# Sums of weights, first norm, last ELU and the place of the h^T reads in a two-layer graph attention kernel

## Chip, cores and metric

The kernel runs on one core of a Trainium2 chip. The metric is the device time of one launch in microseconds (us), the median of three runs. One more run was made under the profiler; every duration below is from that execution.

## What is computed

For each of 64 graphs (256 nodes, 512 channels, float32) two layers are applied, each on the normed and rectified input, each added to it. Layer 0 is gated multi-head attention under an adjacency mask, layer 1 graph attention with one head and an ELU.

```python
# layer 0, h = relu(layernorm(x)), 8 heads of 64
q, k, v = h @ Wq.T, h @ Wk.T, h @ Wv.T
attn = softmax(where(adj != 0, q k^T / 8, -inf)); c = attn @ v
gate = sigmoid(concat([c, h]) @ Wg.T + bg)
x = x + gate * h + (1 - gate) * c
# layer 1, h = relu(layernorm(x))
Wh = h @ W; e = leaky_relu(Wh @ a1 [:, None] + Wh @ a2 [None, :], 0.2)
x = x + elu(softmax(where(adj == 0, -1e9, e)) @ Wh)
```

## The kernel before

Work goes by graph. Graph g is loaded, normed (`p_...`), multiplied to q, k and v, attended (`a_...`), gated and sent through layer 1 (`g_...`). Five graphs are in flight at once: `emit_round(i)` issues, in an order written out by hand, a bit of graph p = i + 1 (its norm, q, k, v and scores), of i (its softmax and weighted sum), of q = i - 1 (gate, residual, second norm), of r = i - 2 (W h, edge logits, output) and of o = i - 3 (ELU and store). The rounds run from -1 to 63, and `emit_end` writes out what is left. Nothing is reordered: each engine executes its instructions in the order in which these functions call them, and so does SyncE (SP), whose queue issues every DMA. An instruction that waits holds all that stand behind it on its engine.

Each 512-wide product is cut by Strassen's scheme (`strassen`, L163): seven products "1" to "7" of half-size blocks are accumulated in three PSUM banks, and steps named "u1", "u2", "u3", "c00" to "c11" take sums off the banks (L190 on VectorE, L192 on ScalarE). The scheme needs sums of token blocks (`token_sums`, L151, on GpSimd, four a call) and, once per weight, sums of weight blocks (`weight_sums`, L108). A weight's four sums are, in their order, the factor of product 7, that of 6, that of 5 (in place) and that of 4. For q and k they run on VectorE ahead of the first graph's product "6"; for v on GpSimd; for the gate's two weights (gh, gc) and for W they are put in a list of 21 `chores` (4 + 4 sums, one scaling of the bias, 8 edge columns L137, 4 sums), which `chore(chores, n)` takes off n at a time at places in the rounds.

What is called h^T is h with channels on partitions. From graph FIRST = 3 on it is made by three steps: VectorE turns 32 x 32 blocks (`turn`, L244), SP writes them to DRAM in four DMAs (`p_send`, L253), and reads them back in four others, in another order (`p_fetch`, L260). For the first three graphs TensorE transposes instead. The attention weights e take the same way: `a_turn` (L391), `a_send` (L397, one write for each of four quarters of a graph), `a_fetch` (L402, four reads for each). In a round the calls that SP sees around the change are: h^T write of p, first, second, third and fourth write of e of i, h^T read of p, first read of e.

x is loaded by `load_graph` (L92) in one DMA, the adjacency by `load_edges` (L98) into a single buffer, so that the next graph's load waits on SP until `p_mask` (L227) has read the one before. At the start SP issues x, the weights q and k, the adjacency and v. The first norm (`p_stats` ... `p_norm`, L201 to L218) takes both 128-row tiles through each step together.

The ELU of layer 1 is made of `g_neg` (VectorE L635: the negative part, out of PSUM), `g_pos` (ScalarE L640 the positive part, L641 the exponential), `g_elu` (L646) and `g_add` (L651, on GpSimd, for the last graphs but one on VectorE). In the last graph `g_add_first` and `g_add_last` (L656, L660) take the place of the last two. In `emit_end`, a = 63, b = 62, c = 61 and o = 60. The tiles of ELU come from the pool `tmp` (5 buffers).

Of the kernel before, what the change touches and what calls it, by code (L numbers as in the profile page):

```python
# [22 lines left out]
def kernel(  # L23
# [65 lines left out]
    def load_graph(g):  # L89
        xt = sb["x"].tile([P, NT, H], F32, tag="t", name=f"x_{g}")  # L90
        at = sb["adj"].tile([P, NT, N], I32, tag="t", name=f"adj_{g}")
        nc.sync.dma_start(xt, x[g].rearrange("(t p) h -> p t h", p=P))  # L92
        graphs[g] = {"x": xt, "adj": at}
        if g > 0:
            load_edges(g)
# [9 lines left out]
        for n in range(2):  # L105
            eng.dma_start(w[:, :, n, :HH], sources[key][:, n * HH:(n + 1) * HH].rearrange("(c p) f -> p c f", p=P))

    def weight_sums(key, eng=None):  # L108

        w = weight[key]  # L110
        t = const.tile([P, 3, 2, w.shape[3]], F32, name=f"w{key}_t")
        b11, b12, b21, b22 = (w[:, r:r + 2, n, :] for r in (0, 2) for n in range(2))
        weight[key] = {1: b11, 2: b21, 3: b22, 4: t[:, 2], 5: b12, 6: t[:, 0], 7: t[:, 1]}
        eng = eng or nc.vector
        return [lambda args=args: eng.tensor_tensor(*args) for args in (
            (t[:, 1], b22, b12, ALU.subtract),
            (t[:, 0], t[:, 1], b11, ALU.add),
            (b12, b12, b11, ALU.subtract),
            (t[:, 2], b21, t[:, 0], ALU.subtract),
        )]  # L120
# [116 lines left out]

    def p_norm(g):
        graphs[g]["h"] = norm_relu(graphs[g], f"l0_{g}")

    def turn(h):

# [381 lines left out]
    def g_out(g, t):  # L624
        s = graphs[g]
        pm = s["po", t] = ps["w"].tile([P, H], F32, tag="t", name=f"po_{g}_{t}")
        for kc in range(NT):
            nc.tensor.matmul(  # L628
                pm, s["egT"][:, t, kc, :], s["wh"][kc][:, :, :HH], start=(kc == 0), stop=(kc == NT - 1)
            )  # L630

    def g_neg(g, t):
        s = graphs[g]
        neg = s["neg", t] = sb["tmp"].tile([P, H], F32, tag="t", name=f"neg_{g}_{t}")
        nc.vector.tensor_scalar(neg, s["po", t], s["rec1"][:, t:t + 1], 0.0, ALU.mult, ALU.min)  # L635

    def g_pos(g, t):
        s = graphs[g]
        pos = s["pos", t] = sb["tmp"].tile([P, H], F32, tag="t", name=f"pos_{g}_{t}")
        nc.scalar.activation(pos, s.pop(("po", t)), AF.Relu, scale=s["rec1"][:, t:t + 1])  # L640
        nc.scalar.activation(s["neg", t], s["neg", t], AF.Exp)  # L641

# [4 lines left out]

    def g_add(g, t):
        s = graphs[g]
        eng = nc.vector if g >= B - 4 else nc.gpsimd  # L650
        eng.tensor_tensor(s["x"][:, t, :], s["x"][:, t, :], s.pop(("pos", t)), ALU.add)  # L651

    def g_add_first(g, t):
# [21 lines left out]
    def emit_round(i):  # L675


        p, q, r, o = i + 1, i - 1, i - 2, i - 3

        def do(fn, g, *args):  # L680
            if 0 <= g < B:
                fn(g, *args)

        def run(fn, g, steps):

            if fn is g_gate and i == 0:
                fn, g = p_qk, p
            elif fn is g_wh and i == 0:
                fn, g = p_v, p
            if 0 <= g < B:  # L690
                if (fn, g) not in products:
                    products[fn, g] = fn(g), set()
                product, done = products[fn, g]
                for step in steps.split():
                    if step not in done:
                        product(step)
                        done.add(step)

        def stats():
            do(p_stats, p + 1, 0)  # L700
            do(p_stats, p + 1, 1)
            do(p_root, p + 1)

        def scores():
            do(a_scores, p, 0)
            do(a_scores, p, 1)
            do(g_out, r, 0)
            do(g_out, r, 1)
            do(a_max, p, 0, 0)
            do(p_bias, p + 1)  # L710
            do(a_exp, p, 0, 0, 0)
            do(a_max, p, 0, 1)
            do(a_exp, p, 0, 0, 1)
            do(p_norm, p + 1)
            do(a_max, p, 1, 0)
            do(a_max, p, 1, 1)
            do(g_fetch_h, q)
            do(a_scale, p, 0, 0)
            do(a_exp, p, 0, 1, 0)
            do(a_exp, p, 0, 1, 1)  # L720
            do(g_neg, r, 0)


        if i == 0:
            do(p_sums, p)
        run(g_gate, q, "1")
        do(g_neg, o, 1)
        do(p_send, p)
        do(g_pos, o, 0)
        run(g_gate, q, "u1")  # L730
        do(a_scale, i, 0, 1)
        do(a_turn, i, 0, 0, 0)
        do(a_turn, i, 0, 0, 1)
        do(a_send, i, 0, 0)
        do(a_exp, i, 1, 0, 0)
        do(a_exp, i, 1, 0, 1)
        do(a_turn, i, 0, 1, 0)
        run(g_gate, q, "6 u2")
        do(a_turn, i, 0, 1, 1)
        do(a_send, i, 0, 1)  # L740
        if i <= B:
            do(g_sums_h, r)
        do(g_elu, o, 0)
        run(g_gate, q, "5")
        do(a_scale, i, 1, 0)
        do(g_pos, o, 1)
        run(g_gate, q, "7 u3 c11")
        do(a_exp, i, 1, 1, 0)
        do(a_exp, i, 1, 1, 1)
        do(a_scale, i, 1, 1, True)  # L750
        do(a_turn, i, 1, 0, 0)
        do(a_turn, i, 1, 0, 1)
        do(a_send, i, 1, 0)
        do(a_turn, i, 1, 1, 0)
        do(g_diff, q)
        run(g_gate, q, "2 c00 4 c10")
        do(g_tanh, q, 0)
        do(a_turn, i, 1, 1, 1)
        do(a_send, i, 1, 1)
        do(p_fetch, p)  # L760
        do(p_mask, p)
        chore(chores, 2)
        run(g_gate, q, "3 c01")
        do(a_fetch, i, 0, 0)
        do(g_mix, q, 0, True)

        run(g_wh, r, "1 u1")
        do(g_tanh, q, 1)
        do(g_mix, q, 0, False)
        run(g_wh, r, "6 u2 5")  # L770
        do(g_mix, q, 1, True)
        run(g_wh, r, "7 u3 c11")
        do(g_mix, q, 1, False)
        chore(chores, 2)
        run(g_wh, r, "2 c00 4")
        if i != 0:
            do(p_sums, p)
        do(g_turn, q)
        do(g_send, q)
        do(a_fetch, i, 0, 1)  # L780
        run(g_wh, r, "c10 3 c01")
        if i == B - 1:
            return
        do(g_fetch, q)
        do(a_fetch, i, 1, 0)

        if i == -1:
            chore(weight_sums("q"), 4)
            chore(weight_sums("k"), 4)
        run(p_qk, p, "1 u1")  # L790
        do(g_edges, r)
        do(g_logits, r)
        do(g_leaky, r)
        run(p_qk, p, "6 u2 5")
        do(g_elu, o, 1)
        do(g_add, o, 1)
        do(g_add, o, 0)
        do(g_store, o)
        do(g_exp, r)
        do(g_turn_e, r)  # L800
        do(g_send_e, r)
        do(g_rec, r)
        run(p_qk, p, "7 u3 c11 2 c00")
        do(load_graph, p + 1)
        if i == -1:
            for key in ("gh", "gc", "1"):
                load_weight(key, nc.sync)
            load_small()
            chores.extend(weight_sums("gh") + weight_sums("gc"))
            chores.append(lambda: nc.vector.tensor_scalar_mul(hbg, hbg, 0.5))  # L810
            chores.extend(edge_columns() + weight_sums("1"))
        chore(chores, 1)
        do(a_fetch, i, 1, 1)
        do(g_fetch_e, r)
        do(g_residual, q, 0)
        run(p_qk, p, "4 c10")
        do(g_residual, q, 1)
        chore(chores, 1)
        run(p_qk, p, "3 c01")
        chore(chores, 1)  # L820
        do(g_stats, q, 0)
        if i == -1:
            chore(weight_sums("v", nc.gpsimd), 4)
            stats()
            scores()
        run(p_v, p, "1 u1 6 u2")
        do(g_stats, q, 1)
        do(g_root, q)
        run(p_v, p, "5 7 u3 c11")
        do(g_bias, q)  # L830
        do(g_norm, q)
        run(p_v, p, "2 c00")
        chore(chores, 1)
        do(g_turn_h, q)
        do(g_send_h, q)
        run(p_v, p, "4 c10")
        chore(chores, 1)
        run(p_v, p, "3 c01")
        chore(chores, 1)
        if i >= 0:  # L840
            stats()
        do(g_sums, i)

        do(a_weigh, i, 0)
        do(a_evac, i, 0)
        do(a_weigh, i, 1)
        do(a_evac, i, 1)
        do(a_sums, i)
        if i >= 0:
            scores()  # L850
        do(p_turn, p + 1)
# [7 lines left out]
    def emit_end():  # L859
# [99 lines left out]
        for t in range(NT):  # L959
            g_elu(b, t)  # L960
            g_add(b, t)
        g_store(b)
        for t in range(NT):
            g_neg(a, t)
            g_pos(a, t)
            g_add_first(a, t)
        for t in range(NT):
            g_add_last(a, t)
            g_store(a, t)

    with tc.manual_schedule(engines={getattr(mybir.EngineType, e) for e in ("PE", "SP", "Pool", "DVE", "Activation")}):
# [3 lines left out]
        load_edges(0)  # L975
        wake_up()
        load_weight("v", nc.sync)
        p_stats(0, 0)
        p_stats(0, 1)
        for fn in (p_root, p_bias, p_norm, p_transpose_pe):  # L980
            fn(0)
        for i in range(-1, B):
            emit_round(i)
            graphs.pop(i - 4, None)
# [33 lines left out]
```

## Time and profile before

| | |
|---|---|
| median of 3 runs | 3174.41 us (3173.53 to 3177.22) |
| the profiled execution's own time | 3178.26 us |
| its span in the profile | 3176.5 us |
| TensorE busy (matmuls) | 3125.6 us, 98% |
| VectorE busy | 2473.4 us, 78% |
| GpSimd, ScalarE busy | 1507.0 us, 1415.1 us |
| DMA | 589.59 MB, 186 GB/s in the mean |
| chain of work that ended last | TensorE 88%, VectorE 5%, DMA 3% |

The profile has a page with busy times, and views that answer questions: who waited for whom, the instructions in order of time (timeline), busy times by stretch. In the timeline a line is: start in us, duration in us (from the first to the last instruction where several are merged), engine, source line, operation, what it writes <- what it reads, shapes, count, and in brackets the engine's idle time before it and what ended that. PE is TensorE's matmuls, PEld its weight loads, DVE VectorE, ACT ScalarE, POOL GpSimd, SPq the issue of a DMA by SyncE. A round is measured here from one graph's first score matmul (L343) to the next graph's. The shortest are 48.29 us; the 60 rounds from 174.10 to 3087.50 us take 2913.4 us.

### The profile page before, as it was taken

The numbers are of one execution on the slowest core, as the hardware profiler recorded it, in microseconds if no ns is written. First come the engines' busy times: TensorE is split into PE (matmuls) and PEld (weight loads), VectorE is DVE, ScalarE is ACT, GpSimd is POOL, SyncE is SP. The second block draws the span as 40 slices with busy tenths as digits, with TensorE's granted clock in tenths as the row PEclk, the third lists the DMA queues.
The fourth block names the chain that finished last, engine by engine and source line by source line (L and its number), as shares of the span: only waits on it lengthen the run. The fifth ranks groups of instructions, "written<-read, shape, count | busy, mean of one in ns | idle before, by whom it ended". The sixth has DMA issues, their size and how long they took to land.

```text
span 3176.5 us, 66771 instructions
## 1 busy us (share of the span) xinstructions
PE 3125.6 (98%) x22768; PEld 2725.1 (86%) x22768; DVE 2473.4 (78%) x6369; ACT 1415.1 (45%) x3977; POOL 1507.0 (47%) x2179
## 2 busy tenths in 40 slices
PE   7899999999999999999999999999999999999997
PEld 6888889888888888898898888888988988888886
DVE  6777877877878778778778787777787787877776
ACT  2443544544435434445445354344454453443443
POOL 3444544545545445445455354454454554544543
PEclk9999999999999999999999999999999999999999
DMA  5577778787787787787777877877878778778772
GB/s 169 155 173 204 181 185 200 185 191 199 177 203 189 176 209 183 183 202 186 193 198 179 199 186 182 208 181 182 203 185 193 197 180 199 189 178 209 184 169 80
DMA packets 1098163, 589.59 MB, mean 186 GB/s; under 512 B 681568, under 2 KB 1024096, under 8 KB 1097824
## 3 DMA queue, kind: packets, MB, share of 16 engines
q1 hardware_dynamic: 1097824, 585.32, 74.4%
q8 instruction: 183, 3.00, 0.4%
q14 instruction: 156, 1.28, 0.1%
HBM read 304.35 MB, written 280.76 MB: 184 GB/s over the span
## 4 chain that ended last, share of the span: by engine, by line
PE 88%; DVE 5%; DMA 3%; POOL 2%; SPq 1%; issue 1%; ACT 1%; DVEq 0%; ACTq 0%; POOLq 0%
PE pmb_qk L179 10%; PE pmb_z L179 9%; PE pma_qk L179 7%; PE pmc_qk L179 7%; PE pc L423 7%; PE ps L343 6%; PE pma_z L179 6%; PE pmc_z L179 6%; PE po L628 6%; PE pmb_v L179 5%; PE pmb_wh L179 5%; PE pmc_v L179 3%; PE pma_v L179 3%; PE pmc_wh L179 3%; PE pma_wh L179 3%; DVE e L358 1%
## 5 line engine op out<-in xcount | busy, mean ns | idle before, releaser
L367 ACT ACTIVATE e<-e,low 128x256 f32<-128x256 f32 x1024 | 506.4, 499 | 66.1 <-DVE low L358 66.1
L209 POOL TENSOR_TENSOR rs_l<-ve_l,mhalf 128x2 f32<-128x2 f32 x128 | 89.2, 697 | 887.5 <-DVE ve_l L205 887.5
L358 DVE CUSTOM_DVE_ANT_0 e<-ps,mask 128x256 f32<-128x256 f32 x1024 | 362.2, 416 | 104.7 <-PE ps L343 104.7
L382 POOL TENSOR_SCALAR e<-e,rec 128x256 f32<-128x256 f32 x768 | 354.5, 482 | 151.5 <-DVE rec L375 101.9
L391 DVE STREAM_TRANSPOSE eb<-e 128x512 f32<-128x512 f32 x512 | 351.4, 696 | 78.0 <-POOL e L382 65.3
L218 ACT ACTIVATE h_l<-x,nb_l,rs_l 128x512 f32<-128x512 f32 x256 | 194.1, 805 | 220.2 <-DVE nb_l L213 126.0
L157 POOL TENSOR_TENSOR S_l<-hT_l 128x256 f32<-128x256 f32 x128 | 93.9, 733 | 397.7 <-DMA hT_l<-there_h 351.6
L423 PE MATMUL pc<-eT,v 128*64 128x256 f32 x2048 | 238.3, 384 | 7.3 <-DMA eT<-there_e 7.1
L343 PE MATMUL ps<-qk 64*128 64x256 f32 x2048 | 240.0, 384 | 0.9 <-DVE qk L190 0.9
L628 PE MATMUL po<-wh,egT 128*128 128x512 f32 x512 | 237.0, 605 | 0.7 <-ACT egT L611 0.7
L651 POOL TENSOR_TENSOR x<-x,pos 128x512 f32<-128x512 f32 x120 | 150.2, 1273 | 184.2 <-DVE pos L646 184.2
L343 PEld LDWEIGHTS ps<-qk 64*128 64x128 f32 x2048 | 194.2, 188 | 45.8 <-DVE ve_l L205 21.5
L423 PEld LDWEIGHTS pc<-eT,v 128*64 128x64 f32 x2048 | 141.6, 137 | 95.6 <-DMA eT<-there_e 17.4
L244 DVE STREAM_TRANSPOSE h_l<-h_l 128x512 f32<-128x512 f32 x246 | 166.5, 696 | 54.7 <-ACT h_l L218 54.7
L367 ACT ACTIVATION_READ_ACCUMULATOR e<-e,low 128x1 f32 x1024 | 194.9, 190 | 0.0
L628 PEld LDWEIGHTS po<-wh,egT 128*128 128x128 f32 x512 | 92.2, 190 | 113.2 <-issue 92.0
L201 DVE BATCH_NORM_STATS2 bs_l<-x 128x6 f32<-128x512 f32 x256 | 172.9, 676 | 6.7 <-DMA x<-in_x_dram 6.6
L466 ACT ACTIVATE z<-z,hbg 128x256 f32<-128x256 f32 x256 | 116.1, 502 | 108.1 <-DVE z L190 108.1
L461 POOL TENSOR_TENSOR d<-hT_l,cT 128x512 f32<-128x512 f32 x128 | 161.0, 1280 | 0.0
L433 ACT COPY cT<-pc 128x512 f32<-128x512 f32 x128 | 74.9, 586 | 189.8 <-PE pc L423 189.8
L179 PEld LDWEIGHTS pma_z<-hT_l,wgh_sb 128*128 128x128 f32 x1024 | 129.2, 192 | 29.6 <-issue 29.6
L179 PE MATMUL pma_qk<-hT_l,wq_sb 128*128 128x128 f32 x1024 | 137.9, 278 | 9.2 <-DMA hT_l<-there_h 7.5
(151 smaller groups left out, 7990.3 us busy)
## 6 DMA issues: line engine op xcount, KB each, us to landing
there_e<-eb SPq DMA_DIRECT2D x256, 512.0 KB, 3.3
eT<-there_e SPq DMA_DIRECT2D x1024, 128.0 KB, 3.9
there_h<-h_l SPq DMA_DIRECT2D x492, 128.0 KB, 3.3
hT_l<-there_h SPq DMA_DIRECT2D x492, 128.0 KB, 3.3
x<-in_x_dram SPq DMA_DIRECT2D x64, 512.0 KB, 4.0
out_dram<-x SPq DMA_DIRECT2D x63, 512.0 KB, 4.2
there_y<-y SPq DMA_DIRECT2D x62, 512.0 KB, 3.3
yT<-there_y SPq DMA_DIRECT2D x248, 128.0 KB, 3.4
```

What stands on the lines that cost most here:

```text
L179: nc.tensor.matmul(bank[key][(slice(None), *cols)], lhsT, rhs, start=first and i == 0, stop=last and i == len(todo) - 1, skip_group_check= ...
L201: nc.vector.bn_stats(bs, s["x"][:, t, :])
L218: nc.scalar.activation(h[:, t, :], s["x"][:, t, :], AF.Relu, bias=s["nb"][:, t:t + 1], scale=s["rs"][:, t:t + 1])
L244: nc.vector.transpose(h[:, t, :], h[:, t, :])
L343: nc.tensor.matmul(psc[jj, i][:, t, :], qk[r:r + DK, 0, jj, t * P:(t + 1) * P], qk[r:r + DK, 1, jj, :], start=True, stop=True,)
L358: nc.vector.tensor_tensor_reduce(s["e", half, jj][:, i, t, :], s["ps", half][jj, i][:, t, :], s["mask"][:, t, :], -SCALE, HUGE, ALU.add, A ...
L367: nc.scalar.activation(e, e, AF.Exp, bias=s["low", half][:, jj, i, t:t + 1], scale=-1.0, accum_out=s["sums", half][:, jj, i, t:t + 1],)
L382: nc.gpsimd.tensor_scalar(e, e, rec[:, i, t:t + 1], 1.0, ALU.mult, ALU.mult)
L391: nc.vector.transpose(s["eb", half, jj][:, :, 4 * i:4 * i + 4, :].rearrange("p b n c -> p n b c"), e)
L423: nc.tensor.matmul(pc[i * DK:(i + 1) * DK, jj, :].rearrange("p (t a c) -> p t a c", t=NT, c=32), s["v"][:, kc, hd * DK:(hd + 1) * DK], eT[ ...
L461: nc.gpsimd.tensor_tensor(d, s["hT"][:, :, js, :], s["cT"][:, :, js, :], ALU.subtract)
L628: nc.tensor.matmul(pm, s["egT"][:, t, kc, :], s["wh"][kc][:, :, :HH], start=(kc == 0), stop=(kc == NT - 1))
```

## The change

Five things are done.

1. x of the first graph is loaded in two DMAs, one for each tile, and a new `p_first` norms tile by tile: statistics, variance and root of tile 0, then of tile 1, then bias and rectified norm of each.
2. The sums for v go to VectorE, behind the first graph's q and k step "c00". Those of q and k are interleaved: two of each, one of each, one of each. The first graph's mask goes behind them.
3. The chores are listed later in round -1, and eight more are taken near the end of round 0.
4. In every round the h^T read goes between the third and the fourth write of e. In round 0 alone the last read of e goes ahead of the load of graph 2.
5. At the end, `g_neg` and `g_pos` of the last graph stand between the two tiles of the ELU of the graph before it, its tiles come from the pool `e`, the addition of the graph before the last goes to GpSimd, and each tile of the last graph is added and stored in one go.

```diff
     def load_graph(g):
...
-        nc.sync.dma_start(xt, x[g].rearrange("(t p) h -> p t h", p=P))
+        for ts in [slice(0, NT)] if g > 0 else [slice(t, t + 1) for t in range(NT)]:
+            nc.sync.dma_start(xt[:, ts, :], x[g].rearrange("(t p) h -> p t h", p=P)[:, ts, :])
...
+    def p_first():
+
+        s = graphs[0]
+        s["h"] = sb["h"].tile([P, NT, H], F32, tag="t", name="h_l0_0")
...
+        for t in range(NT):
+            bs = st.tile([P, 6], F32, tag="bs", name=f"bs_l0_0_{t}")
+            nc.vector.bn_stats(bs, s["x"][:, t, :])
+            nc.vector.bn_aggr(mv[:, t, :], bs)
+            nc.vector.tensor_scalar_add(ve[:, t, :], mv[:, t, 1:], EPS)
+            nc.gpsimd.tensor_tensor(rs[:, t, :], ve[:, t, :], mhalf[:, :1], ALU.pow)
+        for t in range(NT):
+            nc.vector.scalar_tensor_tensor(nb[:, t, :], mv[:, t, :1], -1.0, rs[:, t, :], ALU.mult, ALU.mult)
+            nc.scalar.activation(s["h"][:, t, :], s["x"][:, t, :], AF.Relu, bias=nb[:, t, :], scale=rs[:, t, :])
...
+    def elu_part(name, g, t):
+        if g < B - 1:
+            return sb["tmp"].tile([P, H], F32, tag="t", name=f"{name}_{g}_{t}")
+        part = sb["e"].tile([P, 2, NT, N], F32, tag="t", name=f"{name}_{g}_{t}")
+        return part.rearrange("p a b n -> p (a b n)")[:, :H]
...
     def g_add(g, t):
         s = graphs[g]
-        eng = nc.vector if g >= B - 4 else nc.gpsimd
+        eng = nc.vector if g in (B - 4, B - 3) else nc.gpsimd
...
         do(a_send, i, 1, 0)
+        do(p_fetch, p)
         do(a_turn, i, 1, 1, 0)
...
         do(a_send, i, 1, 1)
-        do(p_fetch, p)
-        do(p_mask, p)
+        if i >= 0:
+            do(p_mask, p)
         chore(chores, 2)
...
         if i == -1:
-            chore(weight_sums("q"), 4)
-            chore(weight_sums("k"), 4)
+            todo = [weight_sums(key) for key in ("q", "k")]
+            for n in (2, 1, 1):
+                for steps in todo:
+                    chore(steps, n)
+            do(p_mask, p)
         run(p_qk, p, "1 u1")
...
         run(p_qk, p, "7 u3 c11 2 c00")
+        if i == 0:
+            do(a_fetch, i, 1, 1)
         do(load_graph, p + 1)
         if i == -1:
...
-            chores.extend(weight_sums("gh") + weight_sums("gc"))
-            chores.append(lambda: nc.vector.tensor_scalar_mul(hbg, hbg, 0.5))
-            chores.extend(edge_columns() + weight_sums("1"))
+            chore(weight_sums("v"), 4)
         chore(chores, 1)
-        do(a_fetch, i, 1, 1)
+        if i != 0:
+            do(a_fetch, i, 1, 1)
...
         if i == -1:
-            chore(weight_sums("v", nc.gpsimd), 4)
             stats()
             scores()
+            chores.extend(weight_sums("gh") + weight_sums("gc"))
+            chores.append(lambda: nc.vector.tensor_scalar_mul(hbg, hbg, 0.5))
+            chores.extend(edge_columns() + weight_sums("1"))
...
         chore(chores, 1)
+        if i == 0:
+            chore(chores, 8)
         if i >= 0:
             stats()
...
         for t in range(NT):
             g_elu(b, t)
             g_add(b, t)
-        g_store(b)
-        for t in range(NT):
             g_neg(a, t)
             g_pos(a, t)
+        g_store(b)
+        for t in range(NT):
             g_add_first(a, t)
-        for t in range(NT):
             g_add_last(a, t)
             g_store(a, t)
...
-        p_stats(0, 0)
-        p_stats(0, 1)
-        for fn in (p_root, p_bias, p_norm, p_transpose_pe):
-            fn(0)
+        p_first()
+        p_transpose_pe(0)
```

## Prediction

> **What bounds the kernel now.** The page comes first. TensorE is busy for nearly all of the span:
>
> ```profile
> span 3176.5 us, 66771 instructions
> PE 3125.6 (98%) x22768; PEld 2725.1 (86%) x22768; DVE 2473.4 (78%) x6369; ACT 1415.1 (45%) x3977; POOL 1507.0 (47%) x2179
> ```
>
> No matmul is removed, so what can be won is TensorE's idle time, some 51 us, and matmuls that run at a lower clock. The view of who waited for whom, for TensorE alone (total, times, longest), shows where that lies:
>
> ```profile
> PE pma_qk L179 <- DMA hT_l<-there_h: 7.5, 9, 1.8
> PE pc L423 <- DMA eT<-there_e: 7.1, 6, 3.1
> PE pmb_qk L179 <- DVE wk_t L115: 4.9, 1, 4.9
> PE pmb_qk L179 <- DVE u_qk L190: 2.8, 1, 2.8
> ```
>
> Line one is spread over the rounds, the others are single events of the first two rounds. The timeline has the third: at 15 to 22 us the sums for v on POOL and those for q and k on DVE run together at 1.7 us each, and once POOL is done the same DVE sum takes 0.68:
>
> ```profile
> 15.41 1.71 POOL L115 TENSOR_TENSOR wv_t<-wv_sb 128x512 f32<-128x512 f32 x1
> 15.92 1.75 DVE L115 TENSOR_TENSOR wq_t<-wq_sb,wq_t 128x512 f32<-128x512 f32 x1
> 21.06 2.08 PE L179 MATMUL pmb_qk<-S_l,wk_t 128*128 128x128 f32 x8 [4.92 <-DVE wk_t L115]
> 22.61 0.68 DVE L115 TENSOR_TENSOR wk_t<-wk_sb,wk_t 128x512 f32<-128x512 f32 x1
> ```
>
> The eight matmuls take 2.08 us, against 1.06 elsewhere. The view by stretch tells why (length, then busy us of PE, PEld, DVE, ACT, POOL; near the end the clock): behind a stretch with 1.24 of 3.41 us busy, TensorE has half the clock for 10.2 us. It happens once more, from 74.6 to 81.4 us, behind the waits for eT.
>
> ```profile
> 13.18:16.59 3.41, 1.24 (x9) 0.97 (x8) 3.38 (x4) 0.59 (x1) 3.41 (x4) 1.00 1.07 364
> 16.60:26.80 10.20, 5.74 (x27) 5.75 (x28) 7.29 (x6) 0.00 (x0) 5.45 (x4) 0.50 1.06 338
> ```
>
> In a round of the middle I read SP's own timeline and TensorE's. The third write of e is issued at 1744.76, the fourth at 1746.50, when VectorE has turned its block; only then the h^T reads go:
>
> ```profile
> 1744.76 0.32 SPq L397 DMA_DIRECT2D there_e<-eb  x1
> ...
> 1746.50 0.32 SPq L397 DMA_DIRECT2D there_e<-eb  x1
> 1746.99 2.60 SPq L260 DMA_DIRECT2D hT_l<-there_h  x4
> ...
> 1752.61 1.13 PE L179 MATMUL pma_qk<-hT_l,wq_sb 128*128 128x128 f32 x8
> ```
>
> The last read lands at 1752.37 (3.3 us after its issue), TensorE wants it at 1752.6: a margin of 0.25 us in nearly every round. Where a read lands up to 2 us late, the round is longer.
>
> At the end, VectorE does both tiles' ELU of graph 62 before it looks at graph 63, whose output ScalarE needs in turn:
>
> ```profile
> 3167.26 0.69 DVE L651 TENSOR_TENSOR x<-x,pos 128x512 f32<-128x512 f32 x1
> 3167.86 0.74 DVE L635 TENSOR_SCALAR neg<-po,rec 128x512 f32<-128x512 f32 x1
> 3168.64 0.69 ACT L640 ACTIVATE pos<-po,rec 128x512 f32<-128x512 f32 x1 [2.38 <-DVE neg L635]
> 3172.08 1.29 DVE L660 SCALAR_TENSOR_TENSOR x<-neg,x 128x512 f32<-128x512 f32 x2
> ```
>
> **What the Trainium skill says.** "SBUF — State Buffer", section "Who interferes with whom": a VectorE instruction with two inputs in SBUF contends with a GpSimd instruction that reads SBUF. The trace agrees: 1.75 against 0.68 us. "TensorE: Matmul & The Clock Gate", section "What's actually happening": the clock is halved after an idle window of about 3.4 us that runs freely. Here 36% busy was not enough to prevent it, so "idle" is to be read loosely; 2.8 us of idleness at 104 us did not trigger it. "DMA: Bandwidth & Descriptors", section "Two DMAs through the same engine are not ordered": the reader has to wait on the writes' semaphore. So the moved reads still wait for the h writes; these land some 16 us into a round, 2 us before the new place.
>
> **The change, part by part.**
>
> *First norm.* x lands at 5.3 us. Half of it should land some 0.9 us earlier (by 3.3 us half its bytes had moved, plus 1.1 us to the semaphore). By the durations of the timeline: statistics 4.4, variance and its sum until 5.5, tile 1 the same until 6.5, roots (0.72) until 7.4, bias, and the two norms (0.76 each) end at 8.4 instead of 9.85. But TensorE's 44 transposes that wake it up run until 8.8, so the h transposes go from 8.8 to 9.85, the VectorE copy ends at 10.2 instead of 11.18. Gain 1.0 us (bounds 0 and 1.4).
>
> *Sums of q and k.* From 10.2, without the mask (0.52 and 0.89 of waiting for the adjacency). While POOL makes the token sums (to 14.5) a sum takes 1.15, after it 0.63: first two of q until 12.6, first two of k until 14.8, the other four until 17.3, mask (0.38) 17.7, step u2 18.4. TensorE: "1" from 10.25 to 12.2, "6" of q 12.7, of k 14.9 to 15.9, "5" until 17.7, "7" at 18.4, behind u2. Before, "7" began at 26.34: 7.9 us gained. The v sums (4 x 0.63 = 2.5) stand on VectorE between c11 (ends 21.8) and c10, whose product ends at 23.95; they end at 24.3. The score matmuls begin at 26.5 (34.76 before). With no weight sum ahead of the statistics the maxima begin 8.6 us earlier. Together with the norm: **8.5**. If the clock is halved again behind 12.4 to 14.9 us, 6.8 to 10 us at half speed take back 3.4 to 5. The later mask holds adjacency 1, and behind it gh, gc, W, on SP until 17.7 instead of 12.6; they are needed at 37 us or later and land by some 31.
>
> *Round 0.* Without x and adjacency ahead of it the last eT lands some 2 us earlier (76.97 before). But VectorE now takes eight more chores before the statistics: 18 instead of 10, + 8 x 0.61 = 4.9 us, so it is done with the chores at 77.0 instead of 72.5, the statistics at 78.9, and the maxima begin at 79.0 against 80.99. The root on GpSimd, which stands ahead of eight token sums, comes 3.3 us later, and so the scaling of e behind these gains 1.1 only. I take **1.5**, bounds 0 and 4 (half clock gone).
>
> *Round 1.* The five chores that stood there (one 1.21, four 0.69) are gone. u_qk ended at 106.54 and TensorE waited 2.78 us for it; it is ready some 2.5 us earlier, and y's write with it, so the next wait (2.27, behind yT) doesn't grow. **2.5**, bounds 1.5 and 3.
>
> *h^T.* The four reads go out at 18.4 into a round instead of 20.2, landing 1.8 us earlier. Behind them on SP stands the fourth write: it goes at 21.0 instead of 19.7, and is read back only at 39.9. Thirteen of the rounds 3 to 62 waited for h^T; their excess over 48.30 us is 2.01 + 0.35 + 0.29 + 0.35 + 0.92 + 0.70 + 1.32 + 1.19 + 0.83 + 0.26 + 0.61 + 1.13 + 1.10 = 11.1 us. The worst read was 2.0 us late, the new margin is 2.05: **11.0** in the profiled execution, bounds 5 and 12. Next late is eT at the end of the round (0.4 once). GpSimd's four token sums move 1.8 us forward with it, onto VectorE's L476.
>
> *End.* neg of tile 0 can go at 3166.0, when its matmuls are done, that of tile 1 at 3167.8; positive parts and exponentials follow at 3166.8 and 3168.6; the last addition ends at 3171.1 instead of 3173.4. The additions on GpSimd (1.27 each) end at 3168.8, ahead of the last store. **2.3**, bounds 1 and 2.6; the cover is ScalarE's idle 2.38 us.
>
> **Sum.** 8.5 + 1.5 + 2.5 + 11.0 + 2.3 = 25.8 off the profiled execution's 3178.26 us. The median of the runs is 3.85 lower, and they differ by 3.7 among themselves, as late h^T reads would make them; so part of these 11 us isn't in the median. I take 9 there: 23.8, and 3174.41 - 23.8 = **3150.6**.
>
> **Rivals.**
> - *The clock falls again at the start.* For it: 12.4 to 14.9 us holds 1.0 us of matmuls. Against it: the work on both sides fills any window of 3.4 us to half or more, and 54% was enough at 40 to 44 us. 3150.6 + 4 = 3154.6.
> - *The h^T reads win nothing*, because late landings come from a busy DMA that delays them at the new place too. Against it: most landings have the same 3.3 us. 23.8 - 9 = 14.8: 3159.6.
> - *Slower: GpSimd's token sums fall on VectorE's two-input steps.* At the new place they run beside L476 and what follows; a step in company takes 1.21 instead of 0.68, + 0.53. From wh's last step (ends 1753.66) to the transpose that needs it (L569 at 1754.47) there are 0.81 us. One such meeting hides there, two cost 0.25; three, 1.59, cost 0.78 in each of 61 rounds, 48 us: 3199. It decides from 1.2 us a round on (0.81 + 23.8 / 61). Against it: the steps after L476 are turns and sums out of PSUM, with one SBUF input.
>
> **Chances.** Forecast 0.66 (own range 3146 to 3155), clock 0.14, no gain from h^T 0.14, slower 0.03, none of these 0.03. The range, 3145 to 3160.5, takes in the first three. A measurement tells about 0.2% (6 us) from no change: faster 0.93, same 0.04, slower 0.03.
>
> **What would show it.** The first score matmul near 26.5 us; DVE sums of weights at 1.2 and 0.65 us, none at 1.7; no half clock before 30 us; waits for hT_l below 1 us in all; rounds at 48.3; wait for u_qk gone; ACT's wait before the last L640 near 0.5. I am wrong if rounds stay uneven, if the chores of round 0 hold the maxima beyond 72.5 us (81 less 8.5), or if TensorE waits for pe L569 in each round.

## The result, and the profile after

| | before | after |
|---|---|---|
| median of 6 runs each, on one chip | 3175.34 us (3173.53 to 3178.37) | 3149.78 us (3148.71 to 3152.68) |
| ratio | | 0.9918, 95% interval 0.9908 to 0.9928 |
| the profiled execution's own time | 3178.26 us | 3152.68 us |
| its span | 3176.5 us | 3150.9 us |

The changed kernel is 0.8% faster: 25.6 us between the medians and as much between the two profiled executions. The prediction was 3150.6 us, 23.8 us off the median.

The page of the changed kernel begins so (span and busy time of each engine):

```profile
span 3150.9 us, 66781 instructions
PE 3118.2 (99%) x22768; PEld 2726.6 (87%) x22768; DVE 2486.6 (79%) x6373; ACT 1419.0 (45%) x3977; POOL 1524.0 (48%) x2178
```

The matmuls are as many as before, and their busy time fell by 7.4 us only: by 3.7 up to the first scores and by 4.5 in rounds 3 to 62, where the clock was full both times, while it grew by 0.8 in rounds 0 and 1. The 4.5 us are not less work. In the record a matmul begins before the end of the one ahead of it, by 0.16 us at the first product with hT_l. Where its read is late this overlap goes, and the product's first matmul is recorded as 0.35 us long instead of 0.27. So part of the waiting stands in the busy time, and the length of a round is the safer measure. The other 18 us are idle time. The view of who waited for whom, for TensorE (total, times, longest):

```profile
PE pc L440 <- DMA eT<-there_e: 6.9, 8, 1.8
...
PE pmb_qk L179 <- DVE wk_t L115: 1.2, 1, 1.2
...
PE pc L440 <- DMA there_h<-h_l: 0.6, 1, 0.6
PE pmb_qk L179 <- DVE u_qk L190: 0.5, 1, 0.5
```

No line names a DMA of hT_l any more (7.5 us before). The wait for wk_t, 4.9 before, is 1.2. That of 2.8 for u_qk, in round 1, is gone; the 0.5 in this list is another one, at the start (at 17.35 below). One wait grew: in rounds 3 to 62 TensorE stood idle for 3.6 us before products with eT, where there had been 0.6 (0.6 of the 3.6 are in the line that names there_h).

The timeline of the start shows the sums and the products that wait for them:

```profile
12.76 1.10 DVE L115 TENSOR_TENSOR wk_t<-wk_t,wk_sb 128x512 f32<-128x512 f32 x1
13.91 1.16 PE L179 MATMUL pmb_qk<-S_l,wk_t 128*128 128x128 f32 x8 [1.21 <-DVE wk_t L115]
15.59 0.68 DVE L115 TENSOR_TENSOR wk_t<-wk_sb,wk_t 128x512 f32<-128x512 f32 x1
17.35 1.13 PE L179 MATMUL pmb_qk<-S_l,wq_t 128*128 128x128 f32 x8 [0.49 <-DVE u_qk L190]
25.61 1.75 PE L360 MATMUL ps<-qk 64*128 64x256 f32 x13 [0.88 <-DVE qk L190]
```

Product "7" begins at 17.35 instead of 26.34, eight matmuls take 1.06 to 1.16 instead of 2.08, and the first score matmul stands at 25.61 instead of 34.76.

In a round of the middle, SP and TensorE show:

```profile
1725.06 0.32 SPq L414 DMA_DIRECT2D there_e<-eb  x1
1725.56 2.73 SPq L277 DMA_DIRECT2D hT_l<-there_h  x4
1728.34 0.60 SPq L414 DMA_DIRECT2D there_e<-eb  x1
...
1733.10 1.05 PE L179 MATMUL pma_qk<-hT_l,wq_sb 128*128 128x128 f32 x8
```

The round began at 1707.27, so the reads now go out 18.3 us into it. The last lands at 23.5, and TensorE wants it at 25.8: the margin of 0.25 us has become 2.3 (1.5 to 2.7 over rounds 3 to 62). The fourth write goes at 21.1 instead of 19.7, as foretold.

The end of the changed kernel, VectorE, ScalarE and GpSimd:

```profile
3142.87 0.99 DVE L669 SCALAR_TENSOR_TENSOR pos<-neg,pos 128x512 f32<-128x512 f32 x1
...
3143.94 1.26 POOL L674 TENSOR_TENSOR x<-x,pos 128x512 f32<-128x512 f32 x1 [0.63 <-DVE pos L669]
3144.59 1.16 DVE L679 TENSOR_TENSOR x<-x,pos 128x512 f32<-128x512 f32 x1
3144.71 0.69 ACT L663 ACTIVATE pos<-po,rec 128x512 f32<-128x512 f32 x1 [0.51 <-DVE neg L658]
...
3147.26 0.69 DVE L683 SCALAR_TENSOR_TENSOR x<-neg,x 128x512 f32<-128x512 f32 x1
```

ScalarE's last wait is 0.51 us (2.38 before). Two of VectorE's steps, beside GpSimd's additions, take 0.99 and 1.16 us; one alone takes 0.69.

Cut at the first score matmul of each graph, the two profiled executions compare so. The excess is what rounds 3 to 62 take beyond 48.29 us each.

| stretch, us | before | after | won | the prediction's term |
|---|---|---|---|---|
| start to first scores | 34.76 | 25.61 | 9.15 | 8.5 |
| round 0 | 44.12 | 41.07 | 3.05 | 1.5 |
| round 1 | 47.92 | 45.46 | 2.46 | 2.5 |
| rounds 3 to 62, excess | 16.00 | 6.71 | 9.29 | 11.0 |
| last scores to end of span | 88.98 | 87.34 | 1.64 | 2.3 |
| sum | | | 25.6 | 25.8 |

Round 2 is the same in both (47.30 and 47.31). TensorE had half the clock for 6.8 us around the end of round 0 in both: from 74.6 to 81.4 us before, and in two stretches after. The view by stretch has the first of them behind a stretch that was busy to 41% (length, busy PE, PEld, DVE, ACT, POOL, then the clock); the second lies in round 1, from 73.0 to 76.4 us.

```profile
59.40:62.80 3.40, 1.38 (x12) 0.69 (x12) 3.40 (x13) 0.59 (x1) 0.00 (x0) 1.00 1.13 216
62.80:66.20 3.40, 2.86 (x14) 1.49 (x16) 3.33 (x9) 0.00 (x0) 0.00 (x0) 0.50 1.05 280
```

### The profile page after: what moved, and what is told of

The parts are those of the page before. It is cut to its first block, busy times and chain, and to the rows that moved or that the text cites. A ratio compares the mean times of both kernels' runs of the same rounds, so it can differ in the third digit from the quotient of the medians.

```text
span 3150.9 us, 66781 instructions
## 1 busy us (share of the span) xinstructions
PE 3118.2 (99%) x22768; PEld 2726.6 (87%) x22768; DVE 2486.6 (79%) x6373; ACT 1419.0 (45%) x3977; POOL 1524.0 (48%) x2178
## 4 chain that ended last, share of the span: by engine, by line
PE 94%; DVE 2%; DMA 2%; SPq 1%; ACT 0%; issue 0%; POOL 0%; DVEq 0%; ACTq 0%
PE pmb_z L179 11%; PE pmb_qk L179 10%; PE pma_z L179 7%; PE po L645 7%; PE pmc_z L179 7%; PE ps L360 7%; PE pma_qk L179 7%; PE pmc_qk L179 7%; PE pc L440 7%; PE pmb_wh L179 5%; PE pmb_v L179 5%; PE pmc_wh L179 3%; PE pma_wh L179 3%; PE pmc_v L179 3%; PE pma_v L179 3%; DMA eT<-there_e 1%
## 5 line engine op out<-in xcount | busy, mean ns | idle before, releaser
L192 ACT COPY qk<-pma_qk 128x512 f32<-128x512 f32 x64 | 37.5, 586 | 236.2 <-PE pma_qk L179 236.2
```

## The experiments

The versions ran in three groups, each together with the kernel before on the same chip, and the ratios are against those runs: its medians were 3178.15, 3179.40 and 3172.19 us. So it differs by 7 us from group to group, and a microsecond between two versions has to be read from the stretches above rather than from the times. The changed kernel ran once more, in the second group:

> The changed kernel itself, beside the runs below. The ratio to the kernel before is 0.990 to 0.993 again; the rounds 3 to 62 hold 4 to 8 us of excess, none behind hT_l.

Measured: 3152.10 us (3150.19 to 3154.45), ratio 0.9915 (0.9902 to 0.9929). First scores at 26.11, rounds 0 and 1 together 86.85 (86.53 in the first profile), excess 7.66 of which 4.06 waits for eT, end 87.33. So the first scores differ by half a microsecond between executions of one kernel, and the excess by one.

### The h^T reads: undone, done alone, and one place earlier

Undone in the changed kernel:

```diff
         do(a_send, i, 1, 0)
-        do(p_fetch, p)
         do(a_turn, i, 1, 1, 0)
...
         do(a_send, i, 1, 1)
+        do(p_fetch, p)
```

> The changed kernel with the h^T reads put back behind the fourth write of e; all else changed. Theory (the reads' margin of 0.25 us was too small, late landings pass on to TensorE): waits of pma_qk for hT_l come back, 7 to 11 us of excess in the rounds 3 to 62, the median some 8 us over the changed kernel's 3149.8, so 3156 to 3160. Rival (late landings are simply rarer in this execution, or are met at the new place too): no waits for hT_l above 1 us in all, 3149 to 3151.

Measured: 3162.79 us (3161.51 to 3164.39), ratio 0.9948 (0.9934 to 0.9961). The excess is 14.86 us, and the view of TensorE's waits has the old line back:

```profile
PE pma_qk L179 <- DMA hT_l<-there_h: 7.0, 11, 1.3
PE pc L440 <- DMA eT<-there_e: 6.5, 6, 1.6
```

The ratio is some 0.3% above that of the changed kernel, about 9.5 us (either ratio is known to about 0.1%). The absolute times that were expected missed, as the kernel before was itself 3 us longer in this group.

Done alone, in the kernel before:

```diff
         do(a_send, i, 1, 0)
+        do(p_fetch, p)
         do(a_turn, i, 1, 1, 0)
...
         do(a_send, i, 1, 1)
-        do(p_fetch, p)
         do(p_mask, p)
```

> The kernel before with one part of the change alone: the h^T reads between the third and the fourth write of e. Theory (the parts are independent; this one is worth the difference of excess, some 8 to 10 us): first scores at 34 to 35 us and the rounds 0 to 2 as before, no waits for hT_l in the rounds, ratio 0.9970 to 0.9980. Rival (the reads win only together with the new start): 0.9990 or more.

Measured: 3166.95 us (3165.86 to 3170.40), ratio 0.9963 (0.9950 to 0.9975), 12.4 us less than the kernel before on that chip. The excess is 4.21 us instead of the 16.00 of the kernel before's profile, so 11.8 are gone there. In its waits hT_l is missing, and those of the start have stayed:

```profile
PE pmb_qk L179 <- DVE wk_t L115: 4.9, 1, 4.9
PE pmb_qk L179 <- DVE u_qk L190: 2.8, 1, 2.8
```

The view of waits names 7.5 us for hT_l in the kernel before, less than what has gone. Counted from the start of one matmul to the start of the next, against the usual step at the same place in the changed kernel, the first two matmuls with hT_l come late by 13.3 us in all over rounds 3 to 62 in the kernel before, by 12.1 with the reads put back, and by nothing in this version and the changed one. The product that waits for the last read of eT comes late by 1.5, 1.5, 2.4 and 5.0 us in these four. So the late h^T reads cost more than the view shows, and with them gone late reads of eT take part of it back.

Within their intervals the two halves add up: this edit is worth 0.37%, all others together (the version before this one) 0.52%, the whole change 0.82 and 0.85%.

One place earlier still, ahead of the third write:

```diff
         do(a_send, i, 0, 1)
+        do(p_fetch, p)
...
         do(a_send, i, 1, 0)
-        do(p_fetch, p)
```

> The changed kernel with the h^T reads one place further forward, behind the second write of e. Theory (2 us of margin were enough; more is worth nothing): SP waits there for the writes of h until 16 us of a round, the reads go at 16.1 to 18.7, the third write 0.9 us later than now, h^T lands at 21.5; no waits for hT_l, the excess of the rounds 4 to 9 us as now, ratio 0.9905 to 0.9930. Rival (GpSimd's token sums, earlier still, meet VectorE's two-input steps, or the writes behind the blocked queue come late): waits of TensorE behind VectorE or more of them behind eT, excess over 12 us, ratio over 0.9940.

Measured: 3149.78 us (3148.70 to 3150.92), ratio 0.9928 (0.9913 to 0.9943). The reads go at 15.9 into a round and land at 21.6; the third write waits behind them until 19.5. No wait for hT_l, excess 3.13 us. Two more microseconds of margin won nothing that shows beside the other versions of this group (excess 1.56 and 2.70): 2.3 us are enough. The earlier place costs nothing either.

### The start: company, order, norm

The sums for v back on GpSimd, at their old place:

```diff
-            chore(weight_sums("v"), 4)
         chore(chores, 1)
...
         if i == -1:
+            chore(weight_sums("v", nc.gpsimd), 4)
             stats()
```

> The changed kernel with the four sums for v back on GpSimd, where the kernel before had them; the sums of q and k stay interleaved. Theory (the two engines' meeting on SBUF is what made the start slow): the last four sums of q and k take 1.6 us instead of 0.68, step u2 comes at 20 instead of 16.5, TensorE waits 3 us more at product 7, and the clock may fall; first scores at 28 to 30 us instead of 25.6, the median 3152 to 3154. Rival (the order of the sums is what counts, the meeting lies beside other work): first scores at 25 to 26.3, since VectorE also has four sums less; 3149 to 3150.5.

Measured: first scores at 30.40, against 25.61 and 26.11. The timeline (this version's lines stand one lower) has the pair of the kernel before again:

```profile
16.11 1.71 POOL L116 TENSOR_TENSOR wv_t<-wv_sb 128x512 f32<-128x512 f32 x1 [1.18 <-DMA wv_sb<-in_L_gnn_Wv_dram]
...
16.61 1.75 DVE L116 TENSOR_TENSOR wk_t<-wk_sb,wk_t 128x512 f32<-128x512 f32 x1
...
18.29 1.48 DVE L228 TENSOR_SCALAR mask<-adj 128x512 bf16<-128x512 int32 x1
...
20.51 1.77 PE L180 MATMUL pmb_qk<-S_l,wq_t 128*128 128x128 f32 x8 [2.92 <-DVE u_qk L191]
```

The last sum of k takes 1.75 instead of 0.68, the mask of one input too is lengthened (0.41 otherwise), "7" comes 3.2 us later, and behind the 2.92 us of waiting it runs at half the clock. That is the mechanism of the prediction. In the time it doesn't show: 3155.72 us (3152.58 to 3157.02), ratio 0.9924 (0.9911 to 0.9936). Rounds 0 and 1 came out at 87.27, the excess at 4.50, 2 us below the changed kernel's.

All four sums of q first, then all four of k, everything else as in the changed kernel:

```diff
-            for n in (2, 1, 1):
-                for steps in todo:
-                    chore(steps, n)
+            for steps in todo:
+                chore(steps, 4)
```

> The changed kernel with all four sums of q ahead of all four of k; those of v stay on VectorE. Theory (the meeting counts, the order little): product 6 of k starts some 1.0 us later (two uncontended sums of q come first), the eighth sum ends at the same time, u2 follows at the same time or up to 0.5 later; first scores at 25.6 to 26.3, the median 3149.8 to 3150.7. Rival (the order is the larger part): first scores at 28 us or later, 3152 or more.

Measured: 3153.01 us (3150.73 to 3157.92), ratio 0.9920 (0.9906 to 0.9933); first scores at 28.67, 3.1 us after the changed kernel's. Some 1.0 of these is a later h^T copy. Product "6" of k waits 2.39 us instead of 1.21. The rest is the clock, in the view by stretch (length, busy PE, PEld, DVE, ACT, POOL, then the clock):

```profile
13.62:17.00 3.38, 0.99 (x9) 0.92 (x9) 3.35 (x5) 0.00 (x0) 1.13 (x1) 1.00 0.45 161
17.01:20.42 3.41, 3.41 (x19) 3.41 (x18) 1.16 (x3) 0.00 (x0) 0.00 (x0) 0.50 0.48 140
```

The same stretch of the changed kernel, whose wait for wk_t lies near 13 us:

```profile
10.41:13.82 3.41, 2.07 (x16) 1.68 (x15) 2.64 (x4) 0.59 (x1) 2.87 (x3) 1.00 1.09 348
13.83:17.24 3.41, 2.94 (x24) 2.75 (x24) 3.37 (x7) 0.00 (x0) 0.00 (x0) 1.00 0.56 197
```

So the rival of the prediction, the clock that falls again, was near: interleaving holds it off here. My theory gave the order less than a microsecond and missed that.

The first norm with both tiles together, x in one load:

```diff
-        p_first()
-        p_transpose_pe(0)
+        p_stats(0, 0)
+        p_stats(0, 1)
+        for fn in (p_root, p_bias, p_norm, p_transpose_pe):
+            fn(0)
```

> The changed kernel with x of graph 0 in one DMA and its norm for both tiles together, as before. Theory: the transposes of h begin 1.3 to 1.5 us later (at 9.2 instead of 7.85, the last seven at 9.9), the copy of h^T ends at 11.2 instead of 9.2, everything behind it 1.5 to 2.0 us later: first scores at 27.2 to 27.6, the median 3151.3 to 3151.8. Rival (the weights' landing bounds the start: wk landed at 11.6 us and VectorE waited for it): 0.5 us or less, 3149.8 to 3150.3.

Measured: 3154.22 us (3150.40 to 3154.55), ratio 0.9919 (0.9905 to 0.9932), which the measurement doesn't tell from the whole change. First scores at 27.21. Over all versions the h^T copy begins at 9.2 us in the mean with the norm by tiles (8.49 to 9.66, ten profiles) and at 10.2 without (9.81 to 10.49, three): 1.0 us.

### The eight chores of round 0

```diff
-        if i == 0:
-            chore(chores, 8)
```

> The changed kernel without the eight chores at the end of round 0, so that round 1 does them as they come. Theory: in round 0 the chores stood ahead of the statistics and made the maxima late, so it ends 0 to 1.5 us earlier; round 1 waits again for u_qk, 2 to 3 us (0.5 in the changed kernel); rounds 0 and 1 together 87.5 to 89 us instead of 86.5. Rival (VectorE has room in round 1, or the wait moves to another place that was late anyway): 86.5 or less.

Measured: 3155.98 us (3154.69 to 3159.16), ratio 0.9928 (0.9916 to 0.9941). Rounds 0 and 1 take 92.84 us together, against 86.53 and 86.85, more than any theory gave. Not all of it is the chores': round 0 had half the clock from 32.7 to 36.2 us, ahead of the edit. The version with the h^T reads put back had that too and took 87.45, so some 5.4 us are theirs. VectorE's timeline shows what the eight had been laid into; without them it waits in round 0 for x:

```profile
68.47 0.69 DVE L201 BATCH_NORM_STATS2 bs_l<-x 128x6 f32<-128x512 f32 x1 [4.29 <-DMA x<-in_x_dram]
...
71.45 0.42 DVE L375 CUSTOM_DVE_ANT_0 e<-ps,mask 128x256 f32<-128x256 f32 x1 [1.08 <-PE ps L360]
```

With them the statistics begin at 67.21 without a wait and the maxima at 69.06. So 4.3 of their 4.9 us were free. In round 1 TensorE's timeline has the wait for u_qk again:

```profile
97.14 1.64 PE L179 MATMUL pmb_qk<-S_l,wq_t 128*128 128x128 f32 x8 [2.78 <-DVE u_qk L190]
```

and the view by stretch half the clock behind it (the column behind the five engines):

```profile
94.20:97.60 3.40, 0.62 (x6) 0.49 (x5) 2.80 (x7) 0.00 (x0) 0.00 (x0) 1.00 0.09 37
97.61:101.02 3.41, 3.41 (x18) 3.41 (x18) 0.49 (x1) 0.00 (x0) 0.00 (x0) 0.50 1.01 261
```

The wait has the same 2.78 us as in the kernel before, where the clock had stayed (the last section says why).

### The end: as before, and with VectorE's additions

The end of the kernel before, all else changed:

```diff
-            g_neg(a, t)
-            g_pos(a, t)
         g_store(b)
         for t in range(NT):
+            g_neg(a, t)
+            g_pos(a, t)
             g_add_first(a, t)
+        for t in range(NT):
             g_add_last(a, t)
```

with the old tiles and VectorE's additions.

> The changed kernel with the end as it was (both tiles of graph 62's ELU first, its additions on VectorE, tiles from tmp). Theory: from the first output matmul of graph 63 to the end of the last addition 9.3 us instead of 7.8, last stretch 88.9 instead of 87.3 us, 1.5 us in the span; in the median 1 to 2 us, at the edge of what the runs can tell. Rival (the last store's landing bounds the end): last stretch 87.3 to 87.8.

Measured: 3150.72 us (3149.84 to 3151.34), ratio 0.9932 (0.9915 to 0.9948). The last addition ends 9.25 us behind the first output matmul of graph 63, the end takes 88.92. In the changed kernel these are 7.77 and 87.34: the new end is worth 1.5 to 1.6 us.

The new order with the additions of graph 62 on VectorE:

```diff
-        eng = nc.vector if g in (B - 4, B - 3) else nc.gpsimd
+        eng = nc.vector if g >= B - 4 else nc.gpsimd
```

> The changed kernel with the two additions of graph 62 on VectorE again, the rest of the new end kept. Theory (on GpSimd they meet VectorE's two-input steps, which lengthens L669 to 0.99 and L679 to 1.16 us; moving them off VectorE wins 1.4 and loses 0.8 of it there): additions 0.69 us each, all two-input steps of the end 0.69, the last addition ends 7.6 to 8.0 us after the first output matmul of graph 63, as now (7.8). Rival (the additions' leaving VectorE is what shortened the end): 8.8 us or more.

Measured: 3149.28 us (3148.62 to 3150.12), ratio 0.9927 (0.9912 to 0.9941); the last addition ends at 7.94, the end takes 87.52. All steps of two inputs are short again, for instance:

```profile
3139.82 0.68 DVE L669 SCALAR_TENSOR_TENSOR pos<-neg,pos 128x512 f32<-128x512 f32 x1
3140.53 0.69 DVE L674 TENSOR_TENSOR x<-x,pos 128x512 f32<-128x512 f32 x1
3141.80 0.68 DVE L679 TENSOR_TENSOR x<-x,pos 128x512 f32<-128x512 f32 x1
```

So GpSimd's two additions, taken off VectorE, win 0.2 us: two steps of 0.69 go, and 0.30 and 0.47 come back by their company; the 0.4 that then remain unseen were probably time in which VectorE waits for ScalarE anyway, which no run took apart. Nearly all of the end's gain is the order.

### The next late transfer: eT ahead of x

The excess that is left belongs to eT, whose last read stands on SP behind the load of the next graph. In round 0 the change had already put it ahead. The same in every round:

```diff
-        if i == 0:
-            do(a_fetch, i, 1, 1)
+        do(a_fetch, i, 1, 1)
         do(load_graph, p + 1)
...
-        if i != 0:
-            do(a_fetch, i, 1, 1)
```

> The changed kernel with the last read of e ahead of the load of the next graph in every round, not in round 0 alone. Theory (with h^T out of the way, late landings of eT behind the load of x are the next thing that TensorE waits for, 3.6 us of idleness in the rounds): eT lands some 3 us earlier in a round, the waits of pc in the rounds vanish, their excess falls from 4 to 8 us to 3 or less, ratio 0.9900 to 0.9915. Rival (the load of x, 1.5 to 2 us later, then comes late for its statistics at 46.0 us of a round and VectorE's maxima with it): waits behind VectorE's low appear, ratio 0.9925 or more.

Measured: 3147.73 us (3147.62 to 3147.91), ratio 0.9901 (0.9886 to 0.9916). It has the lowest ratio of all versions, and its slowest run lies below the changed kernel's fastest on that chip (3150.19). SP's timeline near the end of a round, in the changed kernel:

```profile
1745.25 0.69 SPq L93 DMA_DIRECT2D x<-in_x_dram  x1
1745.99 0.47 SPq L99 DMA_DIRECT2D adj<-in_adj_dram  x1
1746.50 1.89 SPq L419 DMA_DIRECT2D eT<-there_e  x4
```

And in the same round of this version, which began 0.9 us earlier:

```profile
1743.97 2.78 SPq L419 DMA_DIRECT2D eT<-there_e  x4
1746.80 0.43 SPq L93 DMA_DIRECT2D x<-in_x_dram  x1
1747.28 0.47 SPq L99 DMA_DIRECT2D adj<-in_adj_dram  x1
```

The last of these reads lands 43.0 us into the round instead of 45.5; the last product that needs it begins near 47.3. x lands at 44.6 instead of 42.1, and its statistics, at 46.0, don't wait. The excess is 1.01 us, with no wait for eT in rounds 3 to 62.

## Why the prediction was right, step by step

**The first norm** was given 1.0 us by way of the transposes that wake TensorE up, and 1.0 is the mean over the versions. In the two profiles compared above the h^T copy begins 2.0 us apart, at 10.49 and 8.49, which more than covers the 0.65 us that the start won beyond the forecast. The half of x landed earlier than I took (3.4 us, not 4.4), but that lengthened only the wait for those transposes.

**The sums of q and k** came as worked out: "7" at 17.35 (18.4 foretold), sums of 1.1 and 0.68 us, none of 1.7. From the h^T copy to the first scores it is 24.27 us in the kernel before and 17.12 and 16.97 in the two profiles of the changed one; with v back on GpSimd it is 20.74, so 3.6 to 3.8 of the 7.2 us are lost again. What the working did not see is that the order among them was worth about 2 us, most of it by the clock. What then remains, a microsecond or two, no run took apart; the mask, which had held VectorE for 0.52 us and its wait for the adjacency for 0.89 ahead of the sums, now stands behind them. The rival had the right mechanism and the right place, but did not occur.

**Rounds 0 and 1.** This term was mis-sized: 4.0 foretold, 5.5 measured. In round 1 the wait for u_qk is gone as foretold, but that the term is exact (2.46 for 2.5) is in part luck. Over the versions that leave these rounds as the change has them, round 1 took 43.5 to 45.9 us and round 0 40.6 to 43.8, by where stretches at half clock fell; both together took 85.5 to 87.5, so 4.6 to 6.5 us were won. In round 0 the last product with eT begins 39.58 us behind the scores instead of 42.22: 2.6 earlier, where I had taken 2 for the landing, and then took half a microsecond off for the scaling of e. That scaling did start later against the scores (8.94 us instead of 8.02), but it falls in the next round and was not waited for there. The product also took 1.56 instead of 1.98. No run put this read of eT back alone, so its share rests on the timeline. The feared delay of the maxima was covered by VectorE's wait for x.

**h^T** was right in mechanism: the waits named hT_l are gone, and the margin is 2.3 us where 2.05 was foretold. The size for the profiled execution, 11.0, was too large by 1.7, and not because h^T was worth less: its reads had cost 13.3 us, counted from start to start. The working kept "0.4 once" for eT, and with h^T out of the way late eT reads leave TensorE idle for 3.6 and 4.1 us in the two profiles. That eT would be next is what the prediction said; its price was wrong by some 3 us, and putting eT first takes it away. The old margin of 0.25 us was in truth none: in the rounds that waited, too, the product began 0.14 to 0.25 us behind the last landing. The 9 that I took for the median, since part of the late reads should not show there, was if anything too low, as 25.6 us came off it and not 23.8: the one that undid it loses some 9.5, the one that did it alone won 12.4. The rival that the reads win nothing falls with both.

**The end** was mis-sized: 2.3 foretold, 1.5 to 1.6 measured. The working placed GpSimd's additions ahead of the last store and did not ask which steps of VectorE run beside them. Two do, at 0.99 and 1.16 us; the 0.77 us that they are longer are about the difference, though by this sum alone.

**The slower rival**, GpSimd's token sums on VectorE's L476 in every round, did not occur: rounds without a late transfer take 48.29 and 48.30 us, as before. The three waits for pe L586 (1.6 us in all) do not recur in the rounds.

Three errors (+1.5 for the rounds, +0.65 for the start, -2.4 for h^T and the end) nearly cancel; that the sum lies within 0.2 us of the measured one is in part luck.

What stays open: why the excess differs between executions (1.6 to 7.7 us in versions that leave h^T and eT as the change has them). Late reads of eT are its largest part in the worst (counted from start to start, 5.0 of the changed kernel's 6.7 us and 5.8 of 7.7 when it ran again), but why they are late, I have not tried.

## What to carry to other kernels

Where rounds of a bound engine are uneven, take the shortest as the measure and ask who ends the wait in the others; move that transfer on its queue until its margin exceeds its worst lateness, and expect the transfer with the next smallest margin to give back part of it. Lay extra work of an engine where the engine waits for a transfer: eight steps of 0.61 us each cost next to nothing there. Before putting work on an idle engine, look at what the other one executes in those very microseconds, since two additions so moved won 0.2 us.

## What the runs showed of the hardware

The Trainium skill, "TensorE: Matmul & The Clock Gate", section "What's actually happening", says that the clock is halved behind an idle window of about 3.4 us that runs freely. The profiles show how that is to be read. I laid a grid of cells of 3.41 us through the start of a stretch at half clock, over the first 130 us of each of the thirteen profiles. Of the cells at full clock, each that was busy up to 44% was followed by a halved one (36% in the kernel before at 13.2 us, 30% in the version with q first, 18% in the one without the eight chores); of cells between 47 and 51% some were and some not (51% in the changed kernel at 69.6 us was); none above was. Half-clock stretches last 3.4, 6.8 or 10.2 us. So "idle" means here less than about half busy. The matmuls' busy time is not the whole rule: cells of the same 47% near 30 us were followed by half the clock in three versions and not in four, and a round 0 with that stretch took 43.4 to 43.7 us instead of 40.6 to 41.4. And where a wait falls on the grid decides: the same wait for u_qk of 2.78 us lay across two cells in the kernel before (58% and 61%, no halving), and within one of 18% without the eight chores, which was followed by a halved one. An edit that shifts the start by a microsecond can so win or lose a stretch later on.

The other thing not expected is how widely company costs. On VectorE a sum of weights takes 1.10 us beside GpSimd's token sums, a step 0.99 to 1.16 beside additions of 1.27 us, and a sum 1.75 beside sums of 1.71, where each takes 0.68 or 0.69 alone. GpSimd pays too: token sums of 0.72 us take 1.06 and 1.17 there. And it is not only steps of two inputs: beside GpSimd's sums the mask, a tensor_scalar of one input, took 1.48 us instead of 0.41. The Trainium skill, "SBUF — State Buffer", section "Who interferes with whom", names tensor_scalar among the operations that can contend; the prediction had drawn on its two-input rule alone.
